# The last two superchunks' rows stored by SyncE from one tile; three gathers made in place

## The chip, the cores and the metric

The kernel runs on 1 core of one Trainium2 chip. The metric is device time in microseconds (us). Before the change three runs took 4008.17, 4012.63 and 4010.82 us, a median of 4010.82. The change is judged by the same median.

The engines are named as in the profile: PE is TensorE (PEld its weight loads), DVE is VectorE, ACT is ScalarE, POOL is GpSimd, SP is SyncE. A "q" behind an engine (SPq, POOLq) marks its sequencer, which waits, branches and issues DMAs. "L1493" is line 1493 of the kernel.

## The reference, cut to what matters

A two-layer graph attention network (GAT) over 6250 nodes and 200,000 edges sorted by destination, on top of a layer norm, with two residuals:

```python
h = jnp.maximum(_layernorm(x), 0.0)
out = x + gnn(h, src, dst, edge_attr_32)

# one layer; (heads, features) is (4, 64) in layer 0 and (1, 256) in layer 1
te = relu(edge_attr @ We + be) * exp(x @ Wo + bo)[src][:, None]
s2, d2, ea2 = _add_self_loops(src, dst, te, n)       # mean of te per destination
hx = (x @ Wg).reshape(n, h, f)
al = leaky_relu(hx.a_s [s2] + hx.a_d [d2] + (ea2 @ Wge).a_e, 0.2)
al = softmax of al over the edges that share a destination
out = segment_sum(hx[s2] * al, d2) + b
x = relu(out + x)        # layer 0
x = out + x + orig       # layer 1
```

## The kernel before

**Tiling.** The sorted edges are cut into `NS` = 66 superchunks. A superchunk has 24 chunks of 128 edges, the last two have 14 and 13 (`cuts`, `C` = 24). Because the edges are sorted, a superchunk covers a short run of consecutive nodes: about 96 for 24 chunks (32 edges to a node on average). Row p of a result tile belongs to node `base + p - 1`, where `base` is the first destination of the superchunk; row 0 is the node carried over from the superchunk before. Layer 0 runs superchunks 0 to 65 as steps k = 0 to 65, layer 1 runs them again as steps 66 to 131.

**One step.** `gather` issues one indirect DMA on POOL for each chunk (L971): 128 rows of 1 KB or so of the node table `T[l]`, by source index, into `G[:, c, :]`. POOL does next to nothing else after the prologue. `logits`, `links` and `maxima` (DVE, a few PE transposes) make the softmax weights, `scale` (DVE, layer 0) or `scale_rows` (ACT, layer 1) multiplies the rows, `onehots` builds one-hot matrices `S`, and `sums` (PE, L1353) adds the rows up by destination, one product for each chunk, into PSUM `u`. `evict` (ACT, L1358) copies that to `U`, and `finish` merges the self loop on DVE. Meanwhile `rphase1` (L1071 on PE, L1072 on ACT, in two pieces through the one PSUM tile `y`) and `rphase2` prepare the edge attributes of the next step.

**Buffers of the gathers.** There are three buffers for `G`, used in turn by `k % 3`. `gather` normally takes a new tile in the buffer; its first DMA then waits until everything that read the old tile in it is done. A step that has `"own"` set gathers into an existing tile instead, in place, so that each chunk waits only for the readers of that chunk. Before the change step 3 has it (tile `G0` of step 0), and steps 66, 68 and 69 at the change of layers.

**The change of layers.** In layer 0 `rows1` to `rows3` turn a finished superchunk into rows of the next layer's table: transposes (L1443), a copy on ACT (L1445), the product with `wg1` (L471 on PE), bias (L475 on DVE), an exponential of one column (L1455 on ACT) and a store to `T[1]` by SP (L1484). Layer 1's gathers read that table. `ending` writes out by hand the order of the last three superchunks `a`, `b`, `c` of a layer and of the next layer's first, `after`. Its gathers read an early copy `T1e` that lacks the last rows, and `complete` (L1151, L1152) puts the lacking rows in by one-hot products; so POOL goes on with step 66 while `c` is still computed, and waits for `T[1]` only before step 67. `y = self.rphase1(after)` is started early in `ending` (one piece) and finished by `drain(y)` between `rows2(a)`/`rows3(a)` and `rows1(b)`. `warm` issues filler products on PE.

**The end.** In layer 1 `rows3` stores the finished rows `o`. Superchunks below `self.direct` (= NS - 2 = 64) are stored by SP: 112 rows from `min(base, N - 112)`, each store waiting for the one before, since they overlap (L1493). The last two could run past row N, so they are stored by POOL with an indirect DMA of 128 rows and indices `oidx` (L805, L806), whose out-of-range rows are dropped (L1496).

**After the last store.** `general` loads a flag into a register of every engine (L1522) and branches (L1523) over a long fallback path that runs only when the data break an assumption (`checks` adds these up in `bad`; `flag` makes the number in layer 1, superchunk 2). Behind the branch each engine waits for its own last work, SP for its eight DMA semaphores, and POOL for the eight of its indirect DMAs; POOL then runs an instruction INC_SWDGE_SEM. At the end of the program (L1715) SP waits for all semaphores, each engine drains and all meet.

Of the kernel before, what the change touches and what calls it, by code (L numbers as in the profile page):

```python
# [22 lines left out]
F32 = mybir.dt.float32  # L23
BF = mybir.dt.bfloat16
I32 = mybir.dt.int32
AF = mybir.ActivationFunctionType
OP = mybir.AluOpType
# [4 lines left out]
P = 128  # L32
# [3 lines left out]
D = 256  # L36
ED = 32
PH = 64
BIG = 1e38
M = 112  # L40
PAD_DST = 1 << 20
END_DST = 1 << 22
# [37 lines left out]
class Kernel:  # L80
# [396 lines left out]
    def indices(self, wp):  # L477


        nc, cp, a = self.nc, self.cp, self.a  # L480
# [59 lines left out]
        yield  # L540
        self.base_i = cp.tile([1, 3, NS], I32, name="base_i")
        V.tensor_copy(self.base_i[:, 0, :], base[0:1, :])
        V.tensor_scalar(self.base_i[:, 1, :], base[0:1, :], float(N - M), None, op0=OP.min)
        yield
        if NS > 1:
# [30 lines left out]
    def checks(self, qd31, low):  # L576
# [17 lines left out]
        if self.early:  # L594
            V.tensor_scalar(chk[:, 4, NS:], base[0:1, NS - 3:NS - 2], float(N - 2 * P), None, op0=OP.is_lt)
        V.memset(self.bad[:, 0:1], 0.0)
        V.tensor_reduce(self.bad[0:1, 0:1], chk.rearrange("p a b -> p (a b)"), axis=AX.X, op=OP.add)
# [81 lines left out]
    def edges(self, ctx):  # L679
# [12 lines left out]
        self.state = {0: None, 1: None}  # L692
        if len(steps) > 3 and steps[3]["L"].l == 0:
            steps[3]["own"] = self.G0
        self.nodes(steps[0])
# [15 lines left out]
        for k, st in enumerate(steps):  # L711
# [13 lines left out]
            if st["L"].l and (st["s"] == 2 or st["s"] + 3 == self.NS) and not hasattr(self, "flag_i"):  # L725
                self.flag()
            if st["s"] + 3 == self.NS:
                self.ending(st, *steps[k + 1:k + 3], pv, late, steps[k + 3] if k + 3 < len(steps) else None)
                pv = late = None
                continue  # L730
            self.gather(nx)
            st["rows"] = st["L"].l
# [60 lines left out]
    def ending(self, a, b, c, pv, late, after):  # L793

        nc, k = self.nc, a["k"]
        early = after and self.early
        for q in (a, b, c) if after else ():
            q["lag"] = True
# [3 lines left out]
        self.gather(c)  # L802
        for q in () if after else (b, c):
            q["idx"] = idx = self.np_.tile([P, 1], I32, name="oidx")
            nc.vector.tensor_add(idx, self.base_f[:, q["s"]:q["s"] + 1], self.iota_m)  # L805
            nc.vector.memset(idx[0:1, :], 1 << 20)  # L806
# [99 lines left out]
        if after:  # L906
            self.rows3(a)
        drain(y)
        self.rows1(b)
# [11 lines left out]
        if early:  # L921
            self.select(after, 0, 0, 16)
        self.rows3(c)
        if after:
            fill = iter(())
# [99 lines left out]
    def row(self, i, s):  # L1025

        top = (self.N, self.N - M, (self.NS + 1) // 2 * (M + 1) - 1)[i]
        return self.nc.values_load(self.base_i[0:1, i, s:s + 1], engines=(mybir.EngineType.SP,), min_val=0,
                                   max_val=top, skip_runtime_bounds_check_because="destinations are nodes")
# [73 lines left out]
    def lacking(self):  # L1103
# [14 lines left out]
        self.k_lack = self.kps[:, P + 40:P + 42]  # L1118
        V.tensor_scalar(self.k_lack, t[:, 0, :], -1.0, None, op0=OP.add)

    def sources(self, st):
# [357 lines left out]
    def rows3(self, st):  # L1479
# [10 lines left out]
        o, out = st["o"], self.a["out"]  # L1490
        if s < self.direct:
            r = self.row(1, s)
            nc.sync.dma_start(out[ds(r, M), :], o[1:M + 1, :])  # L1493
        else:
            idx = st["idx"]
            nc.gpsimd.indirect_dma_start(  # L1496
                out=out[:, :], out_offset=bass.IndirectOffsetOnAxis(ap=idx[:, 0:1], axis=0), in_=o,
                in_offset=None, bounds_check=self.N - 1, oob_is_err=False)
# [132 lines left out]
def drain(g):  # L1631
    for _ in g:
        pass
# [85 lines left out]
```

## Time and profile before

| what | value |
|---|---|
| median of 3 runs | 4010.82 us (4008.17 to 4012.63) |
| profiled execution, its own time | 4009.49 us |
| its span, first to last instruction | 4007.7 us |
| mean granted TensorE clock | 0.787 |
| POOL | 3000.5 us busy (75%), 3264 instructions |
| PE / DVE / ACT | 2654.4 / 2446.4 / 1120.2 us busy |
| gathers (L971) | 3078, mean 950 ns each |
| DMA | 592.01 MB, mean 148 GB/s |

How to read it. The busy share of POOL is 75%, but an indirect DMA also needs about 0.30 us of issue between two of them, which the profile counts as idle with the releaser "issue". In a timeline row stand the start, the length in us, engine, line, operation, tiles and, in brackets, the idle time of the engine before it and what ended it. A group row gives busy time and mean ns, then that idle time. A row of one line's instructions ("x3: a/b/c, s to e") gives shortest, median and longest duration in ns and the first and last start.

### The profile page before, as it was taken

The page shows a single profiled execution, that of the slowest core. Times are in us where ns is not written, and L with a number is a line of the kernel's source. Part 1 is how long each engine was busy: PE and PEld are TensorE (multiplying, and loading weights), DVE is VectorE, ACT ScalarE, POOL GpSimd, SP SyncE. Part 2 cuts the span into 40 slices and gives each one's busy share as a digit, 9 for nine tenths or more (in the row PEclk, how much of TensorE's full clock was granted, in tenths as well). Part 3 has the DMA queues.
Part 4 walks back from the last instruction along what each step waited for, and adds up shares of the span by engine and source line. Part 5 has one row for each costly group of instructions (what it writes and reads, how often), then busy time and mean ns, then how long its engine had stood idle before and what let it go on. Part 6 is the DMA issues. An engine that isn't in the chain of part 4 may idle for free. (4 is left out here: it accounts for less than half of the span.)

```text
span 4007.7 us, 37932 instructions
## 1 busy us (share of the span) xinstructions
PE 2654.4 (66%) x10018; PEld 1741.3 (43%) x10018; DVE 2446.4 (61%) x6074; ACT 1120.2 (28%) x2676; POOL 3000.5 (75%) x3264
## 2 busy tenths in 40 slices
PE   8777676676666666666786666666565665665665
PEld 6444444444444444444454343343343343343343
DVE  7798877877877877877874443443443443443445
ACT  6211111111111111111124343343343343343341
POOL 6777777777777777777777777777777777777775
PEclk9888888888888888888898777777777777777777
DMA  7555555555555555555555445445445545545553
GB/s 245 139 163 150 154 160 147 152 160 148 151 161 149 151 160 150 151 160 149 153 168 144 132 138 143 134 138 145 132 139 143 134 138 144 132 138 143 133 139 97
DMA packets 248103, 592.01 MB, mean 148 GB/s; under 512 B 65851, under 2 KB 105329, under 8 KB 247643
## 3 DMA queue, kind: packets, MB, share of 16 engines
q0 software_dynamic: 150144, 422.75, 40.8%
q1 hardware_dynamic: 97197, 166.49, 13.0%
q8 instruction: 86, 1.41, 0.1%
q14 instruction: 132, 1.08, 0.1%
q10 hardware_dynamic: 544, 0.28, 0.0%
HBM read 544.19 MB, written 45.46 MB: 147 GB/s over the span
## 5 line engine op out<-in xcount | busy, mean ns | idle before, releaser
L971 POOL DMA_INDIRECT G<-T,src x3078 | 2923.8, 950 | 949.6 <-issue 898.1
L1353 PE MATMUL u<-G,S 128*128 128x270 f32 (+1 forms) x6226 | 1567.4, 415 | 192.1 <-DVE G L1324 190.7
L1353 PEld LDWEIGHTS u<-G,S 128*128 128x128 f32 x6226 | 1275.5, 206 | 483.3 <-DVE G L1324 217.4
L1343 ACT ACTIVATE G<-G,kw 128x256 f32<-128x256 f32 x1512 | 609.0, 496 | 0.0
L1072 ACT ACTIVATE R<-y,webd 128x1024 f32<-128x1024 f32 (+2 forms) x264 | 235.5, 892 | 1274.9 <-PE y L1071 795.2
L1250 PE MATMUL lf<-ident,fb 128*36 128x128 f32 (+1 forms) x132 | 49.8, 377 | 766.2 <-DVE fb L1243 764.0
L1226 DVE TENSOR_TENSOR G<-rt,G 128x96 f32<-128x96 f32 (+1 forms) x132 | 30.3, 229 | 806.7 <-DMA G<-T,src 806.1
L1334 DVE TENSOR_TENSOR G<-G,kps 128x6144 f32<-128x6144 f32 (+3 forms) x79 | 441.0, 5593 | 0.0
L1163 DVE TENSOR_TENSOR S<-kps,loc 128x3072 f32<-128x3072 f32 x132 | 437.6, 3315 | 4.6
L1071 PE MATMUL y<-ea,webd 64*128 64x256 f32 (+1 forms) x1056 | 386.0, 825 | 50.2 <-ACT R L1072 50.2
L1080 PE MATMUL zad<-R,wea 128*64 128x384 f32 (+1 forms) x1056 | 301.7, 712 | 157.8 <-ACT R L1072 157.6
L1250 PEld LDWEIGHTS lf<-ident,fb 128*36 128x36 f32 (+1 forms) x132 | 15.7, 119 | 807.2 <-DVE fb L1243 804.1
L1080 PEld LDWEIGHTS zad<-R,wea 128*64 128x64 f32 x1056 | 86.5, 185 | 418.0 <-ACT R L1072 333.7
L1358 ACT ACTIVATE U<-u 128x270 f32<-128x270 f32 (+1 forms) x131 | 51.5, 393 | 631.6 <-PE u L1353 631.6
L1385 DVE SCALAR_TENSOR_TENSOR mg<-U,mw 128x1 f32<-128x1 f32 x66 | 14.6, 221 | 281.1 <-ACT mw L1383 281.1
L1071 PEld LDWEIGHTS y<-ea,webd 64*128 64x128 f32 x1056 | 123.0, 285 | 122.1 <-ACT R L1072 68.8
L1316 DVE SCALAR_TENSOR_TENSOR G<-U,kw,G 1x257 f32<-1x257 f32 x62 | 29.6, 477 | 184.3 <-ACT G L1343 184.3
L1212 DVE STREAM_TRANSPOSE rt<-zad 128x768 f32<-128x768 f32 (+1 forms) x130 | 126.0, 970 | 5.0 <-PE zad L1198 5.0
L471 PE MATMUL fin<-wg,h1T 128*128 128x260 f32 x264 | 122.6, 611 | 3.6 <-ACT h1T L1445 3.6
L1184 PE MATMUL zad<-a,Q 128*128 128x12 bf16 (+1 forms) x132 | 25.9, 197 | 148.5 <-DVE a L1179 148.1
L1095 DVE TENSOR_TENSOR lb<-lb,kps 128x1536 bf16<-128x1536 bf16 (+1 forms) x68 | 112.9, 1661 | 0.0
L1455 ACT ACTIVATE t1row<-t1row 128x1 f32<-128x1 f32 x66 | 13.4, 203 | 354.1 <-DVE t1row L475 354.0
(231 smaller groups left out, 2349.1 us busy)
## 6 DMA issues: line engine op xcount, KB each, us to landing
G<-T,src POOLq DMA_INDIRECT x3078, 2.8
ea<-in_ea_dram SPq DMA_DIRECT2D x64, 768.0 KB
lb<-locrow SPq DMA_DIRECT2D x64, 384.0 KB
nd<-t1row SPq DMA_DIRECT2D x66, 225.8 KB
tw<-nd SPq DMA_DIRECT2D x66, 225.8 KB
tw<-T SPq DMA_DIRECT2D x66, 117.2 KB
T<-t1row SPq DMA_DIRECT2D x66, 113.8 KB
tw<-in_x_dram SPq DMA_DIRECT2D x66, 112.0 KB
```

What stands on the lines that cost most here:

```text
L471: self.nc.tensor.matmul(ps[:, :L.MW], hT[:, k, :], self.wg[L.l][:, k, :], start=(k == 0), stop=(k == 1))
L971: nc.gpsimd.indirect_dma_start(out=G[:, c, 0:L.TW], out_offset=None, in_=st.get("from", self.T[L.l])[0:self.N, :], in_offset=bass.Indirect ...
L1071: nc.tensor.matmul(y[:, i, :n], self.webd[l][r, :], ea[r, w], start=True, stop=True)
L1072: nc.scalar.activation(R[:, :, w], y[:, :, :n], AF.Relu, bias=self.be[l])
L1080: nc.tensor.matmul(st["zad"][i * PH:(i + 1) * PH, o], self.wea[l][0], R[:, i, w], start=True, stop=False)
L1095: V.tensor_tensor(lb[:, :, :n], lb[:, :, :n], self.k_part.unsqueeze(2).to_broadcast([P, i, n]), op=OP.is_equal)
L1163: nc.vector.tensor_tensor(st["S"][:, c0:c1, :], self.k_iota.unsqueeze(1).to_broadcast(w), self.loc[:, o + c0:o + c1].unsqueeze(2).to_broad ...
L1212: V.transpose(rv[:, :32 * c].rearrange("p (b n) -> p b n", b=2), z.rearrange("p (b n) -> p b n", b=2)[:, :, :16 * c])
L1250: self.nc.tensor.transpose(self.lf[0:e.shape[1], 1:P + 1], e, self.ident)
L1334: nc.vector.tensor_tensor(v, v, pw[:, c0:c1, :].unsqueeze(3) .to_broadcast([P, c1 - c0, H, L.F]), op=OP.mult)
L1343: self.nc.scalar.activation(v, v, AF.Copy, scale=st["w"][:, c:c + 1])
L1353: nc.tensor.matmul(st["u"][:, :L.W], S[:, i, :], G[:, i, 0:L.W], start=(j == 0), stop=(j == c - 1))
```

## The change

1. In layer 1 the last two superchunks are stored by SP. Superchunk 64 (`b`) stores `ML` = 80 rows from `min(base, N - 80)`. Superchunk 65 (`c`) goes through `joined`: two PE products with one-hot matrices `last` put the rows of `b` and `c` in place in one PSUM tile for the nodes N - 80 to N - 1, DVE copies it to SBUF, and SP stores 80 rows at a fixed address. The indices `oidx` and POOL's indirect stores go.
2. `window`, called once after `flag` in layer 1, superchunk 2, builds `last` on DVE (eight small instructions). `base_i` has a fourth row, and `checks` has three more conditions.
3. In layer 0 steps 3, 4 and 5 gather in place, into the tiles of steps 0, 1 and 2. Step 3 did so before.
4. In `ending`, `drain(y)` moves from in front of `rows1(b)` to behind `rows3(c)`.

```diff
+ML = 80
-        self.base_i = cp.tile([1, 3, NS], I32, name="base_i")
+        self.base_i = cp.tile([1, 4, NS], I32, name="base_i")
+        V.tensor_scalar(self.base_i[:, 3, :], base[0:1, :], float(N - ML), None, op0=OP.min)
...
+            V.tensor_scalar(chk[:, 4, NS - 2:NS - 1], base[0:1, NS - 2:NS - 1], float(N - ML), None, op0=OP.is_gt)
+            V.tensor_scalar(chk[:, 4, NS - 1:NS], base[0:1, NS - 1:NS], float(N - ML), None, op0=OP.is_lt)
+            V.tensor_scalar(chk[:, 1, NS - 2:NS - 1], nb[:, NS - 2:NS - 1], float(ML), None, op0=OP.is_gt)
...
-        if len(steps) > 3 and steps[3]["L"].l == 0:
-            steps[3]["own"] = self.G0
...
                 self.flag()
+                if self.early:
+                    self.window()
...
+            if 3 <= k + 1 < 6 and nx["L"].l == 0:
+                nx["own"] = steps[k - 2]["G"]
             self.gather(nx)
...
+        c["before"] = b
...
-        for q in () if after else (b, c):
+        for q in () if after or self.early else (b, c):
             q["idx"] = idx = self.np_.tile([P, 1], I32, name="oidx")
...
         if after:
             self.rows3(a)
-        drain(y)
         self.rows1(b)
...
         self.rows3(c)
+        drain(y)
...
+    def window(self):
+
+        nc, cp, N, NS = self.nc, self.cp, self.N, self.NS
+        V = nc.vector
+        t = cp.tile([P, 3], F32, name="win")
+        self.last = cp.tile([P, 2, ML], F32, name="last")
+        b, c = (self.base_f[:, s:s + 1] for s in (NS - 2, NS - 1))
+        for i, q in enumerate((b, c)):
+            V.tensor_scalar(t[:, i:i + 1], q, float(N - ML), self.iota_m, op0=OP.subtract, op1=OP.add)
+        V.tensor_sub(t[:, 2:3], c, b)
+        V.tensor_scalar(t[:, 2:3], t[:, 2:3], self.iota_m, 0.0, op0=OP.subtract, op1=OP.is_le)
+        V.scalar_tensor_tensor(t[:, 0:1], t[:, 2:3], -4096.0, t[:, 0:1], op0=OP.mult, op1=OP.add)
+        V.memset(t[0:1, 0:2], -1.0)
+        for i in range(2):
+            V.tensor_scalar(self.last[:, i, :], self.k_iota[:, 1:ML + 1], t[:, i:i + 1], None, op0=OP.is_equal)
+
+    def joined(self, b, c):
+
+        nc, N = self.nc, self.N
+        y = self.ps_y.tile([P, 2, 512], F32, name="y")[0:ML, 0, 0:D]
+        for i, q in enumerate((b, c)):
+            nc.tensor.matmul(y, self.last[:, i, :], q["o"], start=(i == 0), stop=(i == 1))
+        o = self.np_.tile([P, D], F32, name="fa", bufs=1)
+        nc.vector.tensor_copy(o[0:ML, :], y)
+        nc.sync.dma_start(self.a["out"][N - ML:N, :], o[0:ML, :])
...
         o, out = st["o"], self.a["out"]
-        if s < self.direct:
+        if self.early and s + 2 == self.NS:
+            r = self.row(3, s)
+            nc.sync.dma_start(out[ds(r, ML), :], o[1:ML + 1, :])
+        elif self.early and s + 1 == self.NS:
+            self.joined(st["before"], st)
+        elif s < self.direct:
```

More of the change, by code (lines that the diff above doesn't have):

```diff
@@ L1025, in row @@
     def row(self, i, s):
-        top = (self.N, self.N - M, (self.NS + 1) // 2 * (M + 1) - 1)[i]
+        top = (self.N, self.N - M, (self.NS + 1) // 2 * (M + 1) - 1, self.N - ML)[i]
         return self.nc.values_load(self.base_i[0:1, i, s:s + 1], engines=(mybir.EngineType.SP,), min_val=0,
```

## The prediction

> **What bounds the kernel now.** I read the page's groups first, then the waits of POOL, then the timeline of each place where POOL waits for something other than its own issue.
>
> ```profile
> L971 POOL DMA_INDIRECT G<-T,src x3078 | 2923.8, 950 | 949.6 <-issue 898.1
> L1226 DVE TENSOR_TENSOR G<-rt,G 128x96 f32<-128x96 f32 (+1 forms) x132 | 30.3, 229 | 806.7 <-DMA G<-T,src 806.1
> POOL G L971 <- issue: 904.2, 2968, 0.3
> POOL out_dram L1496 <- DVE mw L1375: 14.5, 1, 14.5
> POOL G L971 <- PE fin L1443: 4.3, 4, 3.4
> POOL G L971 <- DMA T<-t1row: 2.5, 1, 2.5
> ```
>
> A gather costs 950 ns plus 0.30 of issue, 1.25 us, and 3078 of them are 3850 us of a span of 4007.7. POOL never rests between them except in single waits: 3.4 us once, 2.5 us once, 14.5 at the very end. The second row says that the rest of the kernel waits for the gathers (DVE 806 us at the first use of gathered rows). So a microsecond taken from a wait of POOL in the middle reaches the end, a microsecond taken from another engine in mid-layer reaches nothing, and behind the last gather the remaining chain counts in full. The change touches three such places.
>
> **Part 1, layer 0, steps 3 to 5 in place.** Timeline of POOL and PE around steps 3 and 4, and DVE's first use of gathered rows later on:
>
> ```profile
> 139.07 13.48 PE L1353 MATMUL u<-G,S 128*128 128x270 f32 x48 [0.95 <-DVE G L1334]
> 143.25 0.95 POOL L971 DMA_INDIRECT G<-T,src  x1 [0.30 <-PE u L1353]
> 163.75 12.89 PE L1353 MATMUL u<-G,S 128*128 128x270 f32 x48 [3.39 <-DVE G L1324]
> 172.57 0.95 POOL L971 DMA_INDIRECT G<-T,src  x1 [0.30 <-issue]
> 176.92 0.94 POOL L971 DMA_INDIRECT G<-T,src  x1 [3.40 <-PE fin L1443]
> 359.74 0.26 DVE L1226 TENSOR_TENSOR G<-rt,G 128x96 f32<-128x96 f32 x1 [2.82 <-DMA G<-T,src]
> ```
>
> Step 4's first gather (176.92) stands until step 1's sums end (163.75 + 12.89 = 176.64), since the whole tile has to come free. Step 3, already in place, began at 143.25 while step 0's sums ran on to 152.55: in place, a chunk waits for its own product alone. Step 1's first product is done by 164.3, each later one 0.54 us on, against 1.25 for a gather, so step 4 can begin at 172.57 + 1.25 = 173.82. Gain 176.92 - 173.82 = 3.1 us. Step 5 had no wait, and begins at 204 instead of 207; in place nothing holds it. What is late next: DVE is behind here, and first waits for a gather at 359.74, by 2.82 us; of the 806 us of such waits in all nearly every later step has its part. So DVE feels the 3.1 us a step or two behind that, and POOL does not wait for DVE at all before. Bounds 2.6 to 3.4.
>
> **Part 2, the change of layers.** `drain(y)` leaves PE's and ACT's queues ahead of `rows1(b)`. Rows of the timeline, in order:
>
> ```profile
> 2039.20 1.15 PE L471 MATMUL fin<-wg,h1T 128*128 128x260 f32 x4 [1.96 <-ACT h1T L1445]
> 2040.27 1.13 PE L1071 MATMUL y<-ea,webd 64*128 64x512 f32 x4
> 2040.28 0.42 ACT L1432 ACTIVATE fb<-fb 128x256 f32<-128x256 f32 x1 [1.13 <-DVE fb L1430]
> 2041.45 1.11 ACT L1072 ACTIVATE R<-y,webd 128x1024 f32<-128x1024 f32 x1 [0.41 <-PE y L1071]
> 2041.95 0.17 DVE L1394 TENSOR_TENSOR mw<-mw,mg 128x8 f32<-128x8 f32 x1
> 2042.46 0.38 ACT L1445 ACTIVATE h1T<-fin 128x256 f32<-128x256 f32 x1
> 2042.97 0.16 DVE L1397 TENSOR_TENSOR mg<-U,mw 128x4 f32<-128x4 f32 x1 [0.85 <-ACT mw L1395]
> 2044.07 0.43 DVE L475 TENSOR_TENSOR t1row<-fin,bias 128x260 f32<-128x260 f32 x1 [0.34 <-PE fin L471]
> 2049.08 0.20 ACT L1455 ACTIVATE t1row<-t1row 128x1 f32<-128x1 f32 x1 [1.70 <-DVE t1row L475]
> 2049.71 0.95 POOL L971 DMA_INDIRECT G<-T1e,src  x1 [0.30 <-issue]
> 2053.20 0.94 POOL L971 DMA_INDIRECT G<-T,src  x1 [2.54 <-DMA T<-t1row]
> ```
>
> POOL stands from 2050.66 until `c`'s rows are in `T[1]`; that store follows 2049.08. Its chain runs on DVE. DVE waits 0.85 us for a small exponential on ACT that stands behind the 1.11 us of L1072 and `b`'s copy L1445, then 0.34 us for `b`'s product, which waits for the same copy. Without L1071 in front, `b`'s transposes start when L1432 ends (2040.70), its copy at 2041.2, and the exponential goes right behind DVE's L1394 (2042.12). It then holds DVE up by 0.28 instead of 0.85 (0.04 of hand-over, 0.2 of work), a gain of 0.57. `b`'s product ends at 2042.8, before DVE gets there, so 0.30 of the 0.34 goes as well. Sum 0.87 us, and with it the store and step 67 come 0.87 earlier. The most it could be is 2.24: POOL is busy until 2050.66 and then needs 0.30. The least: nothing, or less if the moved work hurts; it now runs behind `rows3(c)`, where PE has only filler products and ACT nothing, and `rphase2`, its reader, is many microseconds off. Value 0.9, bounds -0.5 to 2.2.
>
> **Part 3, the end.** Rows of the timeline, then of the lines behind the branch (shortest/median/longest ns, first and last start us):
>
> ```profile
> 3979.12 0.94 POOL L971 DMA_INDIRECT G<-T,src  x1 [0.30 <-issue]
> 3991.41 0.32 SPq L1493 DMA_DIRECT2D out_dram<-fb  x1
> 3996.63 0.48 DVE L1465 SCALAR_TENSOR_TENSOR fb<-tw,mw,fb 128x256 f32<-128x256 f32 x1
> 3997.69 1.00 POOL L1496 DMA_INDIRECT out_dram<-fb,oidx  x1 [2.15 <-DVE fb L1465]
> L1523 POOLq COMPARE_BRANCH  x1: 57/57/57, 3998.1 to 3998.1; - x1
> L1523 POOLq INC_SWDGE_SEM  x1: 1268/1268/1268, 4001.1 to 4001.1; - x1
> L1715 POOLq DRAIN  x3: 45/107/4489, 4002.4 to 4007.4; - x3
> L1523 SPq COMPARE_BRANCH  x1: 53/53/53, 3991.8 to 3991.8; - x1
> L1523 SPq EVENT_SEMAPHORE  x8: 17/17/17, 3994.5 to 3995.0; - x8
> L1715 SPq EVENT_SEMAPHORE  x14: 17/28/28, 4002.3 to 4007.6; - x14
> L1715 SPq DRAIN  x3: 7/7/13, 4003.0 to 4007.1; - x3
> ```
>
> Now: `c`'s rows are ready at 3996.63 + 0.48 = 3997.1, POOL stores them from 3997.7, branches at 3998.1, reaches INC_SWDGE_SEM at 4001.1 for 1.27 us, and drains for 4.49 us until 4006.85. SP has been ready since 4003.1. The last 0.85 us are the meeting of the engines. So POOL's close is what ends the span, 8.75 us from its branch.
>
> After: POOL's last work is the gather at 3979.12. Its branch comes at about 3980.6, its drain ends near 3989.4: out of the way. SP is last. From 3997.1: product of `c` (that of `b` is done while `c` is being merged), DVE copy, store, close. Nearest rows for the product and the copy, and for a slow product:
>
> ```profile
> 2062.08 0.60 PE L1151 MATMUL fin<-U,S 128*128 128x260 f32 x2
> 2056.93 1.07 PE L1151 MATMUL fin<-U,S 128*128 128x260 f32 x2
> ```
>
> Product 0.60 (260 columns there, 256 here), copy 0.43 (L475 at 2044.07 reads the same width from PSUM), three hand-overs of 0.05: store issued at 3998.3, 0.32 long as at 3991.41. Its close, from SP's own rows: branch to the first wait behind it 3994.5 - 3991.8 = 2.7, eight waits to 3995.0, then from 4002.3 to 4003.1 the waits and drains of the end, 0.8: together 4.1 us, in which the store lands too (a store by SP at 3991.41 was known to be down by 3994.5). 3998.3 + 0.32 + 0.05 + 4.1 = 4002.8; plus 0.9 for the meeting, 4003.7. Gain 4007.7 - 4003.7 = 4.0. SP is the queue that `b`'s store is moved to: it issues at 3994.3, behind `a`'s (3991.41, down by 3994.5 at the latest), is down by 3997.4 by the same bound, and `c`'s does not wait. The product may take 1.07 if PE has gone slow in the 2.2 us in which it idles; I take 0.60, because after an idle of 1.96 us at 2039.20 PE ran the four passes of L471 in 1.15, the pace of the fast row. Bounds of part 3: 3.0 to 4.5.
>
> [...]
>
> **What costs nothing.** A small instruction and what follows it in the prologue:
>
> ```profile
> L543 DVE TENSOR_SCALAR base_i<-base x1: 176/176/176, 68.6 to 68.6; 1x66 int32<-1x66 f32 x1
> 69.74 0.43 DVE L475 TENSOR_TENSOR trow<-ps,bias 128x266 f32<-128x266 f32 x1 [0.61 <-PE ps L471]
> ```
>
> `base_i`'s extra row is one DVE instruction (176 ns in its neighbour) in the prologue at 68.6, and from 69.7 on DVE waits 0.4 to 0.7 us for PE on each tile; 0.2 us if that cover were gone. The three conditions are of the same kind and smaller, and `window` is eight such instructions, 1.4 us at the most; they run in layers where DVE waits 806 us for gathers.
>
> The four `oidx` instructions that go stood in such a wait too.
>
> **The sum.** 3.1 + 0.9 + 4.0 = 8.0 us off the profiled span, 4007.7 to 3999.7. The profiled execution took 4009.49, 1.8 more than its span and 1.3 below the median 4010.82; I take 8.0 from the median: 4002.8.
>
> **The rivals.** (a) POOL's close stays last. If the 4.49 us drain is not POOL's own time but waits for the program's last store, it follows SP's. That lands by 3998.3 + 3.1 = 4001.4, POOL's waits take it to 4001.7 instead of 4001.1, and part 3 turns to -0.6. Time 4010.8 - 3.4 = 4007.4. For it: nothing else shows what the drain does. Against: no semaphore wait stands at it, and it begins right behind INC_SWDGE_SEM.
> (b) Step 4's wait comes back in place or a step later, because a chunk waits for more than its product. Against: step 3 at 143.25. Time 4002.8 + 3.1 = 4005.9.
> (c) This one goes by the sums of step 66 and the first gather of step 69, which takes over its tile:
>
> ```profile
> 2092.61 10.80 PE L1353 MATMUL u<-G,S 128*128 128x261 f32 x48
> 2113.49 0.95 POOL L971 DMA_INDIRECT G<-T,src  x1 [0.30 <-PE u L1353]
> ```
>
> Slower: PE goes slow at the change of layers, where the moved L1071 leaves its gaps unfilled. The two transposes and products of `b` and `c` (0.44 and 1.15 us each) would double, 3.2 us on the store chain, and `complete`'s 48 pairs of products would stay at 1.07 instead of 0.60, some 17 us more for step 66. Its sums end at 2103.4, 10 us ahead of the gather that takes over its tile; beyond that POOL stands, 7 us. Total 10 against 8.0 gained: 4013. It decides once the slow pairs last past two thirds of `complete`; now they end after about 6 us. For it: slow pairs do occur there. Against: two filler products stay between, and four are ahead of `complete`. [...]
> (d) The data break a new condition and the fallback runs. With 1792 and 1600 edges at 32 to a node, the last two superchunks hold about 56 and 50 nodes; 80 is more than 20 past either. Under 1 in 100.
>
> **How the numbers follow.** Forecast 0.69 (4000.3 to 4005.3 by the bounds of the parts), (a) 0.11, (b) 0.07, (c) with (d) 0.06, better than all bounds 0.07. The range reaches to (a) and takes in 1.5 us of scatter between runs: 3999.8 to 4008. The 0.2% that a measurement of this kernel can tell from no change is 8.0 us, 4002.8: the forecast lies on that line. Half of it and the better case make faster 0.50, the other half with (a) and (b) same 0.44, slower 0.06.
>
> **What would show it.** Step 4's first gather at about 173.8 with a gap of 0.30; the gather after the copy-table ones with a gap near 1.7 instead of 2.54; POOL's drain ending near 3985 on the new scale, SP's branch as the last, and the span ending 5.4 us behind SP's last store instead of 9 us behind POOL's. Wrong if POOL's drain stays at the end, if a new wait over 1 us shows at POOL between 200 and 2000, or if pairs of L1151 stay at 1.07.

## The result, and the profile after

| | before | after |
|---|---|---|
| median | 4010.37 us (4006.77 to 4012.63, 11 runs) | 4002.31 us (3999.23 to 4006.54, 11 runs) |
| profiled execution, its own time | 4009.49 us | 4002.87 us |
| its span | 4007.7 us | 4001.0 us |
| mean granted TensorE clock | 0.787 | 0.788 |

The medians differ by 8.06 us. The ratio of the runs is 0.9984, with a 95% interval of 0.9976 to 0.9991: 3.6 to 9.6 us, 6.4 in the middle. The forecast was 4002.8 us. What follows shows that the total came out near the forecast while two of the three terms did not.

The lines of the changed kernel are shifted: L971 is now L979, L1226 is L1260, L1353 is L1387, L1397 is L1431, L1151 is L1185, L1443 is L1477, L1445 is L1479, L471 is L472, L475 is L476, L1071 is L1079, L1455 is L1489, L791 is L798, L1465 is L1499, L1522 and L1523 are L1561 and L1562, L1715 is L1754. New are L1150 (the one-hot products), L1152 (the copy), L1153 and L1527 (the stores of `c` and `b`).

The groups of the changed kernel (busy, mean ns, idle before and what ended most of it) and the waits of POOL (total, times, longest):

```profile
L979 POOL DMA_INDIRECT G<-T,src x3078 | 2922.9, 950 | 948.1 <-issue 890.2 <-PE u L1387 12.8 <-DVE ade L1249 6.4
L1260 DVE TENSOR_TENSOR G<-rt,G 128x96 f32<-128x96 f32 (+1 forms) x132 | 30.3, 229 | 805.9 <-DMA G<-T,src 805.7
POOL G L979 <- issue: 895.0, 2938, 0.3
POOL G L979 <- ACT G L357: 2.5, 1, 2.5
POOL G L979 <- DMA T<-t1row: 2.5, 1, 2.5
```

POOL is still the bound, with the same 950 ns per gather. Its wait of 3.4 us for PE and the 14.5 us at the end are gone. The wait for `T[1]` before step 67 stands at 2.5 us, as before. A wait for ACT, ahead of step 2, has grown from 0.85 us (by its gap) to 2.5. The change adds one DVE instruction of 0.18 us ahead of it (`base_i`); nearly all of the difference is scatter between executions, which matters below.

**Part 1** in the timeline of POOL:

```profile
114.78 0.94 POOL L979 DMA_INDIRECT G<-T,src  x1 [2.55 <-ACT G L357]
173.86 0.95 POOL L979 DMA_INDIRECT G<-T,src  x1 [0.30 <-PE u L1387]
175.11 0.95 POOL L979 DMA_INDIRECT G<-T,src  x1 [0.30 <-PE u L1387]
```

Step 4 begins at 175.11 with a gap of 0.30. Forecast was 173.8; step 2 began 1.6 us later than before (114.78 against 113.17), and without that it would have been 173.5.

**Part 2**, the change of layers:

```profile
2027.67 6.20 PE L1387 MATMUL u<-G,S 128*128 128x270 f32 x26
2036.34 1.15 PE L472 MATMUL fin<-wg,h1T 128*128 128x260 f32 x4 [2.08 <-ACT h1T L1479]
2038.10 0.66 PE L1477 MATMUL fin<-ident,fb 128*128 128x128 f32 x2 [0.61 <-DVE cnt L1403]
2039.29 2.10 PE L472 MATMUL fin<-wg,h1T 128*128 128x260 f32 x4 [0.53 <-ACT h1T L1479]
2039.54 0.16 DVE L1431 TENSOR_TENSOR mg<-U,mw 128x4 f32<-128x4 f32 x1 [0.28 <-ACT mw L1429]
2041.18 3.59 PE L798 MATMUL u<-ident 128*128 128x512 f32 x4
2041.43 0.43 DVE L476 TENSOR_TENSOR t1row<-fin,bias 128x260 f32<-128x260 f32 x1 [1.11 <-PE fin L472]
2047.17 0.20 ACT L1489 ACTIVATE t1row<-t1row 128x1 f32<-128x1 f32 x1 [1.70 <-DVE t1row L476]
2050.55 0.94 POOL L979 DMA_INDIRECT G<-T,src  x1 [2.54 <-DMA T<-t1row]
2052.00 0.68 PE L1185 MATMUL y<-U,S 128*128 128x260 f32 x2 [0.64 <-DMA U<-T]
```

DVE's wait for the small exponential (2039.54) fell from 0.85 to 0.28 us, to the hundredth as forecast. But `b`'s product (2039.29) now takes 2.10 us instead of 1.14, the two fillers behind it (four passes) 3.59 instead of 1.88, and DVE waits 1.11 us for the product where it had waited 0.34. POOL's wait is 2.54 us, not 1.7.

**Part 3**, the end: the timeline, then the lines behind the branch (shortest/median/longest ns, first to last start):

```profile
3991.75 0.32 SPq L1527 DMA_DIRECT2D out_dram<-fb  x1
3991.87 0.63 PE L1150 MATMUL y<-fb,last 128*80 128x256 f32 x2 [0.68 <-DVE mg L1408]
3994.11 0.48 DVE L1499 SCALAR_TENSOR_TENSOR fb<-tw,mw,fb 128x256 f32<-128x256 f32 x1
3994.65 0.66 PE L1150 MATMUL y<-fb,last 128*80 128x256 f32 x2 [2.15 <-DVE fb L1499]
3995.34 0.42 DVE L1152 COPY fa<-y 80x256 f32<-80x256 f32 x1 [0.75 <-PE y L1150]
3995.79 0.33 SPq L1153 DMA_DIRECT2D out_dram<-fa  x1
L1562 SPq COMPARE_BRANCH  x1: 53/53/53, 3996.2 to 3996.2; - x1
L1562 SPq EVENT_SEMAPHORE  x8: 17/17/17, 3998.7 to 3999.3; - x8
L1754 POOLq DRAIN  x3: 40/107/4324, 3980.9 to 4000.7; - x3
```

POOL's long drain now ends at 3980.9 + 4.3 = 3985.2, with no store of the kernel in flight (SP issued one at 3952.61 and the next at 3988.90). SP branches last. From `c`'s merged rows (3994.59) to the end are 6.4 us instead of 4007.7 - 3997.1 = 10.6.

### The profile page after: what moved, and what is told of

Its sections match the earlier page's. It is cut to its first block, busy times and chain, and to the rows that moved or that the text cites. A ratio compares the mean times of both kernels' runs of the same rounds, so it can differ in the third digit from the quotient of the medians.

```text
span 4001.0 us, 37996 instructions
## 1 busy us (share of the span) xinstructions
PE 2658.1 (66%) x10022; PEld 1738.0 (43%) x10022; DVE 2447.2 (61%) x6083; ACT 1120.3 (28%) x2676; POOL 2997.4 (75%) x3262
## 4 chain that ended last, share of the span: by engine, by line
POOL 31%; DVE 29%; issue 13%; PE 10%; ACT 9%; DMA 9%; DVEq 0%; SPq 0%; POOLq 0%; ACTq 0%
POOL G L979 31%; DVE G L1368 8%; DMA G<-T,src 8%; ACT G L1377 7%; DVE S L1197 4%; PE y L1079 4%; DVE lb L1103 2%; PE u L1387 2%; PE ps L472 1%; DVE m L1316 1%; ACT R L1080 1%; DVE rt L1246 1%; DVE al L1262 1%; DVE al L1264 1%; DVE fb L1277 1%
## 5 line engine op out<-in xcount | busy, mean ns | idle before, releaser
L979 POOL DMA_INDIRECT G<-T,src x3078 | 2922.9, 950 | 948.1 <-issue 890.2
L1387 PE MATMUL u<-G,S 128*128 128x270 f32 (+1 forms) x6226 | 1553.4, 412 | 180.9 <-DVE G L1358 179.1
L1387 PEld LDWEIGHTS u<-G,S 128*128 128x128 f32 x6226 | 1265.9, 205 | 468.0 <-DVE G L1358 205.8
L1260 DVE TENSOR_TENSOR G<-rt,G 128x96 f32<-128x96 f32 (+1 forms) x132 | 30.3, 229 | 805.9 <-DMA G<-T,src 805.7
L1079 PE MATMUL y<-ea,webd 64*128 64x256 f32 (+1 forms) x1056 | 395.1, 842 | 50.3 <-ACT R L1080 50.3
L1419 DVE SCALAR_TENSOR_TENSOR mg<-U,mw 128x1 f32<-128x1 f32 x66 | 14.7, 222 | 281.1 <-ACT mw L1417 281.1
L1079 PEld LDWEIGHTS y<-ea,webd 64*128 64x128 f32 x1056 | 125.3, 290 | 122.9 <-ACT R L1080 69.0
L472 PE MATMUL fin<-wg,h1T 128*128 128x260 f32 x264 | 128.1, 635 | 3.1 <-ACT h1T L1479 3.1
L1489 ACT ACTIVATE t1row<-t1row 128x1 f32<-128x1 f32 x66 | 13.4, 203 | 344.8 <-DVE t1row L476 344.7
```

What stands on the lines that cost most here:

```text
L472: self.nc.tensor.matmul(ps[:, :L.MW], hT[:, k, :], self.wg[L.l][:, k, :], start=(k == 0), stop=(k == 1))
L979: nc.gpsimd.indirect_dma_start(out=G[:, c, 0:L.TW], out_offset=None, in_=st.get("from", self.T[L.l])[0:self.N, :], in_offset=bass.Indirect ...
L1079: nc.tensor.matmul(y[:, i, :n], self.webd[l][r, :], ea[r, w], start=True, stop=True)
L1387: nc.tensor.matmul(st["u"][:, :L.W], S[:, i, :], G[:, i, 0:L.W], start=(j == 0), stop=(j == c - 1))
```

## The experiments

Twelve kernels ran, in three sets of four, each set on one chip. The median of the kernel before, run with each set, was 4803.43, 4007.88 and 4011.36 us. The first set thus fell on a chip that behaves otherwise; it is told first and its times are compared only among themselves.

### First set: one part at a time

**Part 1 alone** (`e1_inplace`):

```diff
-        if len(steps) > 3 and steps[3]["L"].l == 0:
-            steps[3]["own"] = self.G0
+            if 3 <= k + 1 < 6 and nx["L"].l == 0:
+                nx["own"] = steps[k - 2]["G"]
             self.gather(nx)
```

> The kernel before, with layer 0's steps 3 to 5 gathered in place and nothing else. Theory (part 1 alone is worth the wait it removes): no wait of 3.4 us for PE before step 4; step 4's first gather comes 3.1 us earlier against step 3's first than before (30.3 us behind it instead of 33.7), the wait does not return at a later step, and the time is 3.1 us lower than before, 4007.3. Rival (the gather is late next for another reason and the 3.1 us are given back in the middle): the wait is gone but step 131's first gather starts within 1 us of 3964.2 and the time is that of before. Tail and change of layers as before: POOL's drain last, 2.5 us of wait before step 67.

**Part 3 alone** (`e2_end`): all of the change's diff but the lines above and the moved `drain(y)`.

> The kernel before, with the stores of the last two superchunks by SP (one-hot products, conditions, window) and nothing else. Theory (POOL's close of 8.8 us was the end, and it follows POOL's last DMA): POOL's drain ends about 12 us ahead of the end, the span ends 6.4 us behind the merged rows of c instead of 10.6, and the time is 4.0 to 4.2 us lower than before, 4006.3. Rival (POOL's drain waits for the last store of the program): the drain ends within 1 us of the end and the time is within 1 us of before. Steps 4 and 67 wait 3.4 and 2.5 us as before.

**Part 2 alone** (`e3_drain`):

```diff
-        drain(y)
         self.rows1(b)
...
         self.rows3(c)
+        drain(y)
```

> The kernel before, with the drain of the edge-attribute pieces moved behind c's rows at the change of layers and nothing else. Theory of the prediction (the queue order was the cost): the wait before step 67 falls from 2.54 to 1.7 us and the time by 0.9. Theory after seeing the changed kernel (the removed products had kept PE's clock up, and without them the transposes and products of b and c take twice as long): the four passes of L471 of c take 2.1 us instead of 1.15, DVE waits over 1 us for them, the wait before step 67 stays at 2.4 to 2.6 us and the time is that of before within 0.3.

**The changed kernel, `b` by POOL** (`e4_b_pool`):

```diff
-        for q in () if after or self.early else (b, c):
+        for q in () if after else (b,):
...
-            r = self.row(3, s)
-            nc.sync.dma_start(out[ds(r, ML), :], o[1:ML + 1, :])
+            idx = st["idx"]
+            nc.gpsimd.indirect_dma_start(
+                out=out[:, :], out_offset=bass.IndirectOffsetOnAxis(ap=idx[:, 0:1], axis=0), in_=o,
+                in_offset=None, bounds_check=self.N - 1, oob_is_err=False)
```

> The changed kernel, but b's rows are stored by POOL with an indirect store as before, c's through the joined tile by SP. Theory (POOL's close, from its branch over INC_SWDGE_SEM to the end of its drain, takes about 9 us from its last DMA, whatever that DMA is): POOL's store of b begins at about 3991.8 on the changed kernel's scale, its drain ends near 4001.1, and the span ends near 4002, 1 us later than with SP's store, with POOL last. Rival (the drain waits for stores still under way and is short without them): the drain is shorter than 2 us and the span stays at the changed kernel's, ended by SP.

| kernel | median | ratio to before, 95% interval |
|---|---|---|
| before | 4803.43 us | |
| `e1_inplace` | 4822.55 | 1.0036 (1.0022 to 1.0050) |
| `e2_end` | 4800.82 | 0.9998 (0.9989 to 1.0007) |
| `e3_drain` | 4800.42 | 0.9996 (0.9987 to 1.0005) |
| `e4_b_pool` | 4819.28 | 1.0035 (1.0021 to 1.0049) |

Of the times only those of `e1_inplace` and `e4_b_pool` are clear, and both went up; `e1_inplace` was expected 3.1 us lower. On this chip POOL is not the bound. PE's group of sums in `e2_end`, and the waits of POOL there:

```profile
L1387 PE MATMUL u<-G,S 128*128 128x270 f32 (+1 forms) x6226 | 1845.3, 443 | 1318.2 <-issue 1126.5
POOL G L979 <- PE zad L1218: 349.2, 62, 7.7
POOL G L979 <- PE u L1387: 187.5, 39, 10.9
```

PE idles 1318 us in front of its sums, 1126 of them for nothing that the profile shows ("issue"); before, on the usual chip, the same group had 192 us. POOL then waits for PE in most steps, and a gather that begins earlier buys nothing. Why part 1 then costs 19 us, and in `e4_b_pool` much the same, shows at steps 2 to 6. First `e1_inplace`, then `e2_end`, which gathers in place in step 3 alone:

```profile
211.54 1.16 POOL L971 DMA_INDIRECT G<-T,src  x1 [4.80 <-PE u L1353]
225.10 0.47 DVE L1260 TENSOR_TENSOR_SCAN cl<-fl,cl,lf 4x129 f32<-4x129 f32 x1 [6.97 <-remote]
234.32 2.08 PE L1071 MATMUL y<-ea,webd 64*128 64x512 f32 x4 [6.94 <-issue]
236.32 0.35 DVE L1277 TENSOR_TENSOR fb<-flpen,lf 128x192 f32<-128x192 bf16 x1 [8.91 <-remote]
250.02 11.97 PE L1353 MATMUL u<-G,S 128*128 128x270 f32 x48
308.24 0.94 POOL L971 DMA_INDIRECT G<-T,src  x1 [26.89 <-PE fin L1443]
```

```profile
223.15 0.35 DVE L1311 TENSOR_TENSOR fb<-flpen,lf 128x192 f32<-128x192 bf16 x1
232.96 7.25 PE L1387 MATMUL u<-G,S 128*128 128x270 f32 x19 [4.55 <-issue]
291.06 0.95 POOL L979 DMA_INDIRECT G<-T,src  x1 [5.05 <-PE zad L1218]
```

With step 4 in place its gathers start at 211.5 instead of 221.8 and run on while PE and DVE work on step 2; just then both stand for 7 and 9 us without a producer that is late ("issue", "remote"). The sums of step 2 begin at 250.0 instead of 233.0, step 6, which needs a whole tile free, waits 26.9 us instead of 5.1, and begins 17 us later. What the two stood for is not shown by any run here.

Three other things hold on this chip too. `e3_drain` has a slow product, 2.10 us, but it is `b`'s and not `c`'s as expected (`c`'s takes 1.14), and from `c`'s sums to its table row it is no faster than `e1_inplace` and `e2_end`, 12.40 us against 12.43; its wait before step 67 is 37 us, for the late sums, and says nothing of part 2. `e2_end` needs 4800.8 - 4794.2 = 6.6 us from `c`'s rows to the end, against 10.4 in `e1_inplace`: part 3's mechanism, with POOL out of the way, though its time cannot tell them from nothing. And `e4_b_pool` shows POOL's close with another last DMA:

```profile
4807.38 1.02 POOL L1527 DMA_INDIRECT out_dram<-fb,oidx  x1 [33.21 <-DVE mw L1409]
4811.17 0.33 SPq L1153 DMA_DIRECT2D out_dram<-fa  x1
L1564 POOLq INC_SWDGE_SEM  x1: 1248/1248/1248, 4810.2 to 4810.2; - x1
L1756 POOLq DRAIN  x3: 40/107/4407, 4811.5 to 4816.5; - x3
```

From the store (4807.38) to the end of the drain (4811.5 + 4.4 = 4815.9) are 8.5 us, 4.4 of them the drain, as 4.49 before and 4.32 after, where nothing was in flight. In none of these three profiles did the drain wait for a store. The 1 us that I expected on the end came out as 0.2: SP was ready at 4815.8, just ahead.

### Second set, on a chip where before takes 4007.88 us

**Part 1 alone**, once more (`f1_inplace`, the edit of `e1_inplace`):

> The kernel before with layer 0's steps 3 to 5 in place and nothing else, once more, since the four runs above fell on a chip on which the kernel before takes 4803 us. Theory (what part 1 is worth depends on who is late): where PE and DVE run ahead of the gathers, as in the profile of before, step 4's first gather comes 31.5 us or less behind step 3's last-but-one chunk without a wait, the 3.4 us do not come back, and the time falls by about 3 us; where PE's and DVE's instruction stalls make the gathers wait for sums, the gathers of steps 4 and 5 run on through the time in which POOL stood before, and the time rises by 15 to 20 us. Rival (part 1 costs on every chip): the time rises on both.

**The changed kernel, with PE's half of the moved piece as filler** (`f2_split`):

```diff
-    def rphase1(self, st):
+    def rphase1(self, st, split=False):
...
+            if split and a:
+                yield
             nc.scalar.activation(R[:, :, w], y[:, :, :n], AF.Relu, bias=self.be[l])
...
-        y = self.rphase1(after) if after else iter(())
+        y = self.rphase1(after, True) if after else iter(())
...
         self.rows1(a)
+        next(y, None)
         self.rows2(a)
```

> The changed kernel, with the PE half of the moved second edge-attribute piece issued between a's transposes and a's product, where PE idles 2.08 us, and its ACT half left behind c's rows. Theory (without these products PE's clock fell, and the slow transposes, products and fillers of b and c ate the 0.9 us of part 2): L472 of b takes 1.15 us instead of 2.10, the four fillers 1.9 instead of 3.6, DVE's wait before b's bias falls from 1.11 to under 0.3 us, and the wait before step 67 falls from 2.54 to between 0.9 and 1.7; time 1 to 1.5 us under the changed kernel. Rival (PE's slow stretch comes at its own time and not from the missing products): b's product still takes 2.1 us and the wait stays at 2.3 to 2.6.

**The changed kernel, `c`'s store by ACT** (`f3_act`):

```diff
-        nc.sync.dma_start(self.a["out"][N - ML:N, :], o[0:ML, :])
+        nc.scalar.dma_start(self.a["out"][N - ML:N, :], o[0:ML, :])
```

> The changed kernel, with c's last store issued by ACT's queue instead of SP's. Theory (the end is SP's branch of 2.5 us and its waits, which begin only behind its last store, while ACT's branch takes 0.4 us): SP branches behind b's store, 3 to 4 us earlier, and only the landing of c's store is left; the span ends 3 to 3.5 us behind the last store's issue instead of 5.2, a gain of about 2 us on the changed kernel. Rival (the landing of the store and its receipt take as long as SP's branch did): the span ends 5 us or more behind the issue, no gain.

**The changed kernel itself** (`f4_after`):

> The changed kernel itself, as the measure for the two variants above on the same chip. If the chip is like that of the result: 8 us under the kernel before, 2.5 us of wait before step 67, POOL's drain 16 us ahead of the end. If it is like that of the four runs before: 12 to 19 us above the kernel before, with the loss between step 4 and step 8 and nowhere else.

### Third set, on a chip where before takes 4011.36 us

**The split piece, and fillers at the end** (`g1_fill`, on top of `f2_split`):

```diff
             nc.tensor.matmul(y, self.last[:, i, :], q["o"], start=(i == 0), stop=(i == 1))
+            if i == 0:
+                self.warm(2, self.ps_1, "u", [P, 512])
```

> The changed kernel with the split piece of the earlier variant, and two filler products on PE between b's and c's one-hot products at the end. Theory (PE goes slow in the 2.15 us in which it idles there, so that c's pair takes 1.03 to 1.14 us in some executions): c's pair takes 0.60 to 0.66 us, the span ends 6.3 to 6.5 us behind c's merged rows and not 6.8 to 7.1, sums of c to c's table row 11.6 us as in the earlier split; time 0.2 to 0.5 us under the split variant, 2 to 3 under the changed kernel. Rival (the clock is already down when the fillers begin): the fillers take 0.9 us each, c's pair stands behind them and begins over 0.3 us after c's rows are ready; no gain or a loss of up to 1 us.

**The same with `c`'s store by ACT** (`g2_fill_act`, the edit of `f3_act` on top):

> As the variant with the fillers, and c's store by ACT's queue. Theory: the span ends 4.5 us behind the store's issue as in the earlier ACT variant, against 5.1 to 5.2 with SP, so 0.6 to 0.7 us under the variant with the fillers alone. Rival (ACT's branch took 2.56 us there by chance and 0.45 in the changed kernel is its rule): ACT's branch takes under 1 us and the span ends 3.5 to 4 us behind the issue.

**The changed kernel without part 1** (`g3_no_inplace`, the edit of `e1_inplace` undone):

> The changed kernel without part 1 (step 3 alone in place, as before). Theory (part 1 is worth 3.2 us where POOL is the bound): step 4 waits 3.4 us for PE again and starts 33.6 us behind step 3 instead of 30.4; time 3 us above the changed kernel. If the chip is one of those on which the sums are late: time 15 to 20 us under the changed kernel. Rival (the 3.2 us are lost again in the layers): the wait is there and the time is that of the changed kernel.

**The changed kernel again** (`g4_after`):

> The changed kernel again, on the chip of the three above. Theory: L472 of b takes 2.1 us, sums of c to c's table row 13.2 to 13.5 us; the step-67 wait is 2.3 us or more and grows by as much as the sums of c end later than 16 us behind step 66's first gather. Rival (the slow stretch is there by chance): L472 of b takes 1.15 us and the chain 11.6.

| kernel | median | ratio to before, 95% interval | from c's sums to its table row | wait before step 67 | c's one-hot product | c's rows to the end |
|---|---|---|---|---|---|---|
| before, profiled | 4010.37 | | 12.43 us | 2.54 us | | 10.6 us |
| after, profiled | 4002.31 | 0.9984 (0.9976 to 0.9991) | 13.50 | 2.54 | 0.66 us | 6.4 |
| `f1_inplace` | 4007.10 | 0.9996 (0.9987 to 1.0005) | 12.42 | 2.50 | | 10.2 |
| `f4_after` | 4004.00 | 0.9984 (0.9975 to 0.9993) | 13.53 | 5.06 | 1.03 | 7.1 |
| `f2_split` | 4001.31 | 0.9981 (0.9972 to 0.9990) | 11.57 | 2.25 | 1.14 | 6.8 |
| `f3_act` | 4003.31 | 0.9987 (0.9978 to 0.9996) | 13.16 | 2.30 | 1.14 | 6.2 |
| `g4_after` | 4004.64 | 0.9985 (0.9976 to 0.9994) | 12.39 | 2.29 | 1.05 | 6.9 |
| `g3_no_inplace` | 4005.95 | 0.9987 (0.9978 to 0.9996) | 12.39 | 2.51 | 1.14 | 7.1 |
| `g1_fill` | 4003.36 | 0.9981 (0.9972 to 0.9990) | 11.64 | 3.34 | 0.66 | 6.4 |
| `g2_fill_act` | 4002.41 | 0.9979 (0.9969 to 0.9989) | 11.72 | 0.86 | 0.66 | 6.1 |

The fourth column runs from the end of the last product of L1353 for `c` to the end of `c`'s L1455 (before: 2030.63 + 6.22 to 2049.08 + 0.20; after: 2027.67 + 6.20 to 2047.17 + 0.20). The changed kernel's ratio is 0.9984, 0.9984 and 0.9985 in three sets: 6.4 us is a better measure of the change than the 8.06 of the first medians; the medians of the two later measurements, `f4_after` and `g4_after`, lie 3.9 and 6.7 us under those of before.

**Part 1** stands: the wait is gone wherever the three steps are in place. But its size is not fixed. Step 4's and step 2's first gathers in `g3_no_inplace`, where step 4 is not in place:

```profile
112.56 0.94 POOL L979 DMA_INDIRECT G<-T,src  x1 [1.97 <-ACT G L357]
174.48 0.94 POOL L979 DMA_INDIRECT G<-T,src  x1 [1.89 <-PE fin L1477]
```

Here POOL loses 1.97 us ahead of step 2 and only 1.89 ahead of step 4; in the profile of before it was 0.85 and 3.40. The sums are alike, 3.9 and 4.3. These are the only two profiles of these chips with a wait ahead of step 4, so this is a reading and not a rule: a POOL that has waited longer ahead of step 2 waits less at step 4, since PE is done at its own time. Among the nine other profiles of these chips the wait ahead of step 2 lay between 0.85 and 2.55, in six of them at 1.59 or more: the profile of before had the smallest wait ahead of step 2 and so the largest gain to offer. That wait goes with PE's granted clock. PE works almost without a pause in the 20 us ahead of step 2 (19.15 us busy in the profiles of before and of the changed kernel), and its clock came back from 0.50 to 1.00 9.9 us behind step 1's first gather in the profile of before, 13.2 us behind it in that of the changed kernel; the other eight lie between, nearly in the order of their waits. `f1_inplace` gained 1.6 us by its ratio (-2.0 to 5.2), and `g4_after` is 1.3 us under `g3_no_inplace` by the medians, with overlapping intervals: no time here shows part 1 clear of nothing, only the traces do.

**Part 2.** In all seven profiles where the products of L1071 (four passes) follow `a`'s product or fill the gap ahead of it (before, `e1`, `e2`, `f1`, `f2`, `g1`, `g2`), `b`'s product takes 1.14 us; in all seven where they come behind `c` (after, `e3`, `e4`, `f3`, `f4`, `g3`, `g4`) it takes 2.10. So the slow stretch is not chance, and the granted clock says what it is. In the clock records of these fourteen traces the granted clock is 1.00 or 0.50, and within a trace its changes lie whole multiples of 3.41 us apart (in the trace of before 345 intervals between changes, in that of the changed kernel 343, all within 2 ns of a multiple of 3413.3 ns). Cut into the stretches of that measured grid, from 100 us behind the start to 20 us ahead of the end, the traces show when the clock fell: stretches at full clock with less than 1 us of busy PE were all followed by half the clock (2058 of 2058, among them 155 of 155 before and 157 of 157 in the changed kernel), those with 1.75 us or more hardly ever (38 of 6285; 3 of 477 and 1 of 470). Three such stretches, two of the changed kernel and then one of `f2_split` (start and end, length, busy us of PE, PEld, DVE, ACT and POOL, granted clock, DMA share, GB/s):

```profile
2034.37:2037.79 3.42, 1.15 (x4) 0.68 (x4) 2.80 (x11) 1.72 (x5) 2.74 (x3) 1.00 0.86 226
2037.79:2041.20 3.41, 2.57 (x7) 1.81 (x8) 2.01 (x14) 1.35 (x5) 2.50 (x4) 0.50 0.97 397
2038.19:2041.60 3.41, 1.90 (x9) 0.78 (x6) 2.81 (x12) 1.96 (x6) 2.50 (x4) 1.00 1.00 313
```

Between `c`'s sums and its row the emptiest stretch has 1.15 to 1.55 us of PE work in the seven profiles with the products behind `c`, and the clock falls in all of them; in the other seven it has 1.80 to 2.17, and the clock stays. It is down for two stretches, 6.8 us, in `after`, `f3` and `f4`, where the chain takes 13.2 to 13.5 us, and for one, 3.4 us, in `e3`, `e4`, `g3` and `g4`, where it takes 12.4. So `g4_after` had the slow product that was expected of it but not the chain of 13.2 to 13.5. `f2_split`, with the products back in PE's gap and ACT's half still behind `c`:

```profile
2031.78 5.65 PE L1390 MATMUL u<-G,S 128*128 128x270 f32 x24
2037.75 1.13 PE L1080 MATMUL y<-ea,webd 64*128 64x512 f32 x4
2039.77 1.15 PE L472 MATMUL fin<-wg,h1T 128*128 128x260 f32 x4 [0.90 <-ACT h1T L1482]
2042.47 1.14 PE L472 MATMUL fin<-wg,h1T 128*128 128x260 f32 x4 [0.53 <-ACT h1T L1482]
2043.45 1.88 PE L798 MATMUL u<-ident 128*128 128x512 f32 x4
2043.78 0.43 DVE L476 TENSOR_TENSOR t1row<-fin,bias 128x260 f32<-128x260 f32 x1
2048.80 0.20 ACT L1492 ACTIVATE t1row<-t1row 128x1 f32<-128x1 f32 x1 [1.70 <-DVE t1row L476]
```

The chain takes 2049.00 - 2037.43 = 11.57 us, 0.86 less than before: the 0.87 of the prediction, once PE stays fast. POOL's first gather from `T[1]` comes 14.7 to 15.1 us behind `c`'s sums in the three profiles with the split (`f2`, `g1`, `g2`), against 16.3 to 16.4 in `before` and `f1_inplace`; what it gains beyond the chain is a shorter landing of the store (3.1 us from its issue to that gather in `f2_split`, 3.9 before). The wait before step 67 is not shorter by as much. In `f2_split` step 65's sums ended 17.6 us behind step 66's first gather (before 16.3), in `f4_after` 18.8, and there POOL stood 5.06 us; in `g2_fill_act` 15.9, and it stood 0.86. The scatter of 3 us in when PE ends, which I have not explained, is larger than part 2.

**Part 3.** The product of `c` (two passes) is slow, 1.03 to 1.14 us, in five of the eight profiles without fillers, and `c`'s rows are then 6.8 to 7.1 us from the end with SP's store, 6.4 to 6.7 with a fast one. The clock decides here too: in the five it fell to 0.50 between 0.8 us before the product's start and 0.15 us behind it, in the other three not before 0.9 us behind it. The product stands behind 2.15 us of idle PE (3.03 in `f4_after`), and where the 3.41 us grid falls in that differs from one execution to the next. With two fillers it is 0.66 in both profiles (`g1_fill`, `g2_fill_act`): the last stretch of the grid that ends before the product does then has 2.5 and 2.7 us of PE work, against 0.4 to 1.4 in the five where it took over 1 us. ACT's store saves less than the 2 us that I expected: `f3_act` ends 4.5 us and `g2_fill_act` 4.9 us behind the store's issue, SP's variants 5.1 to 5.5. In `f3_act`:

```profile
L1562 ACTq COMPARE_BRANCH  x1: 54/54/54, 3996.5 to 3996.5; - x1
L1562 ACTq EVENT_SEMAPHORE  x1: 17/17/17, 3999.0 to 3999.0; - x1
L1562 SPq EVENT_SEMAPHORE  x8: 17/17/17, 3993.9 to 3998.0; - x8
L1754 SPq EVENT_SEMAPHORE  x14: 17/28/306, 3998.1 to 4000.0; - x14
```

ACT's branch takes 2.5 us here, in the changed kernel 0.4 (3993.1 to 3993.5 in the same rows of that profile). But that is not what kept the gain small. SP, which had branched at 3991.4, still had to wait for `c`'s store, issued at 3995.5, and its waits for the DMA semaphores run to 3998.0; in the waits that follow it stood only 0.31 us for ACT. DVE, which branches behind its copy, reached its first wait at 3998.6. So without ACT's branch the end would come about 0.3 us earlier, and the rival of `f3_act`, the landing of the store, was nearer the truth.

The variants `f2_split`, `g1_fill` and `g2_fill_act` have medians 2.7, 1.3 and 2.2 us under the changed kernel of their own set. All point the same way; none is clear of the intervals by itself.

## Why the prediction was right, and where it was not

**What bounds the kernel.** Right on the chips it was read from: what POOL gained stayed. Step 4's first gather came 1.81 us earlier than before (175.11, 176.92), step 131's 2.55 (3961.60, 3964.15). On the chip of the first set the bound was PE, and the change, but for `b`'s store, was 16 us slower (`e4_b_pool`). Nothing in the profile of before could have told that, and the range did not hold it.

**Part 1: 3.1 us.** The mechanism was right and the size belonged to one execution. "Step 4 can begin at 173.82" held to 0.3 us against the start of step 2. The term measures 1.6 us by the ratio of `f1_inplace`, within -2.0 to 5.2, and the two waits seen at step 4 are 3.40 and 1.89 us; the bounds of 2.6 to 3.4 took POOL's lead over PE as given, when the wait ahead of step 2, 0.85 us in that profile, scatters up to 2.55.

**Part 2: 0.9 us.** This step failed where it said of the moved work that "PE has only filler products" where it goes. What it left behind was missed: the four products of L1071 were themselves the filler, and without them PE's clock was 0.50 for 3.4 or 6.8 us of the chain. The forecast's 0.57 on the exponential and 0.30 on the product were both there in `f2_split`, and in the change the slow product took them back: 12.39 to 13.53 us for the chain, against 12.43. The term is between 0 and -1.1 us at `c`'s row, and at POOL's first gather from `T[1]`, 16.4 us behind `c`'s sums before and 15.9 to 16.7 in the changed kernel, about nothing. The rival (c) had this mechanism, but at 10 us for the whole of `complete`; its pairs began at 0.68 us (2052.00) and went on at 0.60, while it was those of before that fell to 1.07 (2056.93).

**Part 3: 4.0 us.** Right in kind and size. POOL's drain ends at 3985.2 (forecast near 3985), the span ends 5.2 us behind SP's last store (forecast 5.4), and rival (a) fell with the 4.32 us drain that had nothing to wait for. The product was the choice that I made wrong: 0.60, from one fast row after an idle of 1.96 us. In the runs without fillers it was slow in five of eight, with 1.03 to 1.14 us. PE's idle ahead of it does not decide: it is 2.15 us in the changed kernel, with 0.66 us, and in `g3_no_inplace`, with 1.14. By these traces it is the busy time within the stretch of the 3.41 us grid ahead of it that does: 0.4 to 1.4 us in those five, 1.62 in the changed kernel, 2.5 and 2.7 with the fillers. Part 3 is then 3.1 to 4.2 us, by 10.2 to 10.6 before and 6.4 to 7.1 after.

**The sum.** 1.6, about 0 and 3.1 to 4.2 make 4.7 to 5.8 us, against 6.4 by the ratios (3.6 to 9.6). The forecast of 8.0 counted the largest step-4 wait and a part 2 that did not come. That the median fell half a microsecond from the forecast is luck: by the medians of the two later measurements the change gains 3.9 and 6.7 us, not 8.06. One sum of the prediction was off as well: the bounds of its parts add up to gains of 5.1 to 10.1 us, which makes 4000.7 to 4005.7 and not 4000.3 to 4005.3.

## What to carry to other kernels

A wait seen in one profile is the difference of two chains. Before counting it, see what the earlier waits of the same engine were in that execution: what one takes, the next can give back (0.85 and 3.40 us in one profile here, 1.97 and 1.89 in another). When work is moved off PE's queue in a stretch full of gaps, split it: leave the products where they keep the clock up (`b`'s product took 1.14 us with those of L1071 there, 2.10 without), and move only what blocks the other engine's queue. And see what the close of the engine that issues the program's last DMA takes: here POOL's took 8.75 us from its branch and SP's 5.2 us from its last store, and keeping POOL's indirect DMAs out of the last 10 us was worth 3 to 4 us. Before the next step there, see which other engine is ready just ahead of it; behind SP's close stood the store's landing and DVE's branch, and a change of queue gained little (4.5 and 4.9 us from the store's issue to the end, against 5.1 to 5.5).

## What was unexpected of the hardware

- One of the chips ran the kernel before in 4803 us, 20% longer, with the same 950 to 953 ns per gather (`e1_inplace`, `e2_end`). There PE and DVE stood for several us at a time without a late producer, up to 9 us at step 2 in `e1_inplace`; ahead of PE's sums it was 1126 us in all in `e2_end`.
- How long the store to `T[1]` took went with the gathers around it. From its issue to the first gather that it released: 3.9 us where POOL's last gather from `T1e` began 0.40 us behind the issue (before, 2049.31 to 2053.20; `f1_inplace` and `g3_no_inplace` the same), 3.5 at 0.28 us (`g4_after`), 3.0 to 3.2 where it began ahead (after, 2047.40 to 2050.55), 2.7 where POOL had stood for 30 us (first set). In `g2_fill_act`, with gathers 0.02 and 1.27 us behind the issue, it was 3.1, so the rule is not that simple.
- From the taken branch to the next instruction on its queue SP took 2.7 us before, 2.5 in the changed kernel and in `f3_act`, 2.8 in `g2_fill_act` and 2.9 in `e4_b_pool`; DVE took 2.8 to 3.1 in the same five profiles, and ACT 0.4 to 0.5 or, with the last store on its queue (`f3_act`, `g2_fill_act`), 2.5 and 2.7. What decides it is open.
